# Layer 3's attention by two heads and a batch element, with projections between its steps and layer 2's last steps among the first of them

## The chip, the cores and the metric

The kernel runs on one core of a Trainium2 chip. The metric is the device time of one execution in microseconds: the median of three runs of the kernel before is 2154.16 us (2153.61 to 2156.42). The core's engines work side by side, each in its own order: TensorE (PE, its weight loads are PEld), VectorE (DVE), ScalarE (ACT), GpSimd (POOL), and SyncE (SP), which issues transfers.

## What is computed

Four layers of gated cross-attention and feed-forward on x, of shape (2, 1024, 256), with a context of 2 x 64 rows. The change lies between layer 2's attention and the end of layer 3's. The part of the reference that bears on it:

```python
x = x + tanh(g_xattn[2]) * _L2_xattn_ref(_layernorm(x), ctx, ctx, mask, ...)     # 16 heads of 16
x = x + tanh(g_ffn[2]) * _L2_ffn_ref(_layernorm(x), weight_q, weight_scale, bias)
x = x + tanh(g_xattn[3]) * _L3_xattn_ref(ctx, _layernorm(x), ...)
x = x + tanh(g_ffn[3]) * _L3_ffn_ref(_layernorm(x), ...)

# _L2_ffn_ref: each row of the normed x is quantised to int8
amax = max(abs(x2d), -1); x_scale = maximum(amax, 1e-6) / 127
x_q = clip(round(x2d / x_scale), -128, 127)
out = (x_q @ weight_q.T) * x_scale * weight_scale + bias

# _L3_xattn_ref(x=ctx, latents=normed x): 8 heads of 64
xn, zn = layer_norm(x, ...), layer_norm(latents, ...)
q = (zn @ Wq) heads; kv_in = concatenate([xn, zn], axis=1)      # 64 + 1024 keys
k, v = (kv_in @ Wk) heads, (kv_in @ Wv) heads
alphas = softmax(q * 64**-0.5 @ k.T)                             # 1024 queries x 1088 keys
return (alphas @ v) joined @ Wout
```

## The kernel before, in words

x lies in SBUF as 16 tiles of 128 rows (tiles 0 to 7 are batch element 0, tiles 8 to 15 are batch element 1). Inside the stages looked at here TensorE's order is the order of the program (`manual_schedule`); the orders of the other engines are made by a scheduler when the program is built. PSUM has eight banks. `banks(s, A)` sets how many are in the ring "s" (one bank each, taken in turn by `ps`) and how many tiles of two banks there are in "A" (`psA`); `evac` copies a bank to SBUF, in turn by DVE and by ACT.

**Layer 2's attention** (`ctx_attn`, from L530) runs one tile per step n. Its scores (L554) stand on TensorE at step n, the transposes of its exponentials two steps later, the product with the values three steps later, and the update of x four steps later. Steps of the layer that follows hang on it through `then`, a list of (lag, function): function f runs for tile n - lag at step n. For layer 2 these are the functions of `l2_ffn`: norm (statistics and, for every fourth tile, the normed rows xn of four tiles), quantised (the maximum, the scale, q on ACT, the clip on POOL, xq on ACT, and the bias added to x on POOL), turn (qtr, L1751, the transposes of four xq tiles, every fourth step), product (acc, the product with the int8 weights in bf16, and x updated), norms (two norms in one, on POOL, then zn of four tiles), and zturn (tr, L188, the transposes of four zn into zT). The lags are 4, 7, 8, 12, 13, 14. The loop ends at step 20; what is left of `then` is returned as a flat list of calls, `rest`.

**Layer 3's attention** is set up in `l2_l3_xattn`. `projected(b, o)` (from L1838) makes q, k, v of all eight heads for batch element b: with 512 columns of zT at a time, a product for each of four head pairs of q and of k (prj, L204), and v by tiles of 128 rows and 512 columns (v, L1858); kc and vc are the keys and values of the context, kcb a block form of kc in which two heads share one 128-wide operand. It is a generator; the projections of batch element 0 are run one by one between the calls of `rest` (L1872 to L1880), and those of batch element 1 stand between the two calls of `l3_heads`.

`l3_heads` (from L1888) takes one batch element in 32 steps: groups of two query tiles, and in a group four head pairs by two tiles. Step n does, on TensorE: the scores s of two heads (L1928, two tiles of "A", all of it), the first or second half of the values' product for an earlier tile pair (po, L1963), and the transposes et of the exponentials of step n - 1 (L1951, four banks of "s"). DVE takes the maxima (L1936, L1937) and half of the et copies, ACT the exponentials (L1938) and the other half. Once a group: `context` (sc, scores against the context, L1911), `shares` (L1975 to L1980: POOL adds, ACT takes the exponential, DVE sums it to r and inverts), `spread` (ecT; POOL copies r to rb, wide; R, L2001), `joined` (pc, L2016, and two DVE operations on half a group at a time), and `out` (wo, L2030: for each query tile four products added up in PSUM, then `add_gated`, L236, onto x). The pipeline runs out after 32 steps and starts again for the other batch element. After it layer 3's feed-forward takes the norm of all of x (L172 to L176).

Of the kernel before, what the change touches and what calls it, by code (L numbers as in the profile page):

```python
# [11 lines left out]
F32 = mybir.dt.float32  # L12
# [8 lines left out]
P = 128  # L21
# [19 lines left out]
class Net:  # L41
# [488 lines left out]
    def ctx_attn(self, pool, kbd, vblk, queries, extra, wo, gate, some=None, then=(), take=None):  # L530
# [57 lines left out]
        with tc.manual_schedule(engines={mybir.EngineType.PE}):  # L588
# [17 lines left out]
            partial(f, n - k)  # L606
            for n in range(last, NT + max([0] + [k + 1 for k, _ in then]))
            for k, f in then if 0 <= n - k < NT
# [335 lines left out]
    def l1(self, take, taken, back):  # L944
# [4 lines left out]
        with tc.tile_pool(name="l1f", bufs=1, side="right") as pool:  # L949
# [9 lines left out]
            with tc.tile_pool(name="l1a", bufs=1, side="right") as fp:  # L959
                es = ExitStack()  # L960
                f = self.l1_front(fp, es.enter_context(tc.tile_pool(name="l1q", bufs=1, side="right")), rows)
                rest = self.l1_xattn(f["steps"], take)
                taken()
                self.l1_attention(u, f, rest, es.close, ln2, oh, hbuf)
# [730 lines left out]
    def l2_ffn(self, pool, lw, zT):  # L1695
# [94 lines left out]
        return (4, norm), (7, quantised), (8, turn), (12, product), (13, norms), (14, zturn)  # L1790


    def l2_l3_xattn(self, late, take, taken):
# [4 lines left out]
        with ExitStack() as es:  # L1798
# [34 lines left out]
            qp = es.enter_context(tc.tile_pool(name="l3p", bufs=1))  # L1833

            kcb = qp.tile([P, 4, 2, L], F32, tag="kcb", name="kcb")
            nc.gpsimd.memset(kcb, 0.0)

            def projected(b, o):  # L1838

                zb = zT[:, :, b * S : (b + 1) * S]  # L1840
                cb = cT[:, :, b * L : (b + 1) * L]
                qT = o["qT"] = qp.tile([P, 4, S], F32, tag="qT", name="qT")
                kT = o["kT"] = qp.tile([P, 4, S], F32, tag="kT", name="kT")
                v = o["v"] = qp.tile([P, KM, 512], F32, tag="v", name="v")

                vc = o["vc"] = qp.tile([P, 512], F32, tag="vc", name="vc")
                for h in range(2):
                    t = slice(512 * h, 512 * h + 512)
                    for m in range(4):
                        self.project_T(wq[:, :, ts(m, P)], zb[:, :, t], qT[:, m : m + 1, t], scale=D3X**-0.5)  # L1850
                        yield
                        self.project_T(wk[:, :, ts(m, P)], zb[:, :, t], kT[:, m : m + 1, t])
                        yield
                    for t in range(4 * h, 4 * h + 4 + h):
                        p = self.ps("v")
                        for k in range(DC):
                            src = zb[:, k, ts(t, P)] if t < KM else c2[:, k, b]
                            nc.tensor.matmul(p, src, wv[:, k, :], start=k == 0, stop=k == DC - 1)  # L1858
                        self.evac(v[:, t, :] if t < KM else vc, p)
                        yield  # L1860
                for m in range(4):
                    p = self.ps("kc")
                    for k in range(DC):
                        nc.tensor.matmul(
                            p[:, :L], wk[:, k, ts(m, P)], cb[:, k, :], start=k == 0, stop=k == DC - 1
                        )
                    for h in range(2):
                        r = slice(64 * h, 64 * h + 64)
                        self.evac(kcb[r, m, h, :], p[r, :L])

            o = {}
            with tc.manual_schedule(engines={mybir.EngineType.PE}):  # L1872

                steps = projected(0, o)
                for n, f in enumerate(rest):
                    f()
                    if n >= 2:
                        next(steps, None)
                for _ in steps:
                    pass  # L1880
            fs.close()
            hp = es.enter_context(tc.tile_pool(name="l3h", bufs=1))
            self.l3_heads(hp, 0, o["qT"], o["kT"], kcb, o["v"], o["vc"], wo)
            for _ in projected(1, o):
                pass
            self.l3_heads(hp, 1, o["qT"], o["kT"], kcb, o["v"], o["vc"], wo)

    def l3_heads(self, pool, b, qT, kT, kcb, v, vc, wo):  # L1888
# [5 lines left out]
        KM, GS = S // P, 8  # L1894
        self.banks(s=3, A=2)
        G = S // 256
        e, eT, po, grp = {}, {}, {}, {}

        def context(g):

            q = grp[g] = dict(
                sc=pool.tile([P, 2, H3X, L], F32, tag="scs", name="scs", bufs=2),
                nmc=pool.tile([P, 2, H3X], F32, tag="nmc", name="nmc", bufs=2),
                nm=pool.tile([P, 2, H3X], F32, tag="nm", name="nm", bufs=2),
                rs=pool.tile([P, 2, H3X], F32, tag="rs", name="rs", bufs=2),
                oT=pool.tile([P, 4, 256], F32, tag="oT", name="oT"),
            )
            for t in range(2):
                p = self.ps("sc")
                for c in range(4):  # L1910
                    nc.tensor.matmul(  # L1911
                        p[:, ts(c, P)], qT[:, c, ts(2 * g + t, P)],
                        kcb[:, c].rearrange("p h l -> p (h l)"), start=True, stop=True,
                    )
                nc.scalar.copy(q["sc"][:, t].rearrange("p h l -> p (h l)"), p)
# [419 lines left out]
```

## Time and profile before

| | us |
|---|---|
| median of three runs | 2154.16 |
| the profiled execution | 2174.95 |
| its span, first to last instruction | 2173.2 |
| layer 2's attention, first to last scores on TensorE | about 1190 to 1273 |
| first and second projection of batch element 0 on TensorE | 1309.35, 1312.03 |
| first head scores of batch element 0 | 1380.63 |
| projections of batch element 1 on TensorE | 1650.67 to about 1694 |
| first head scores of batch element 1 | 1698.01 |
| layer 3's last wo begins | 1959.13 |
| first normed row xn of the feed-forward | 1966.10 |
| mean granted clock of TensorE, share of full | 0.923 |

How to read the profile: the page gives each engine's busy time and the costliest groups of instructions, with the mean duration and what ended the idle time before them. The view by stage gives the busy time of each engine between two times, with the granted clock. The timeline lists instructions in order of time: start, duration, engine, line, operation, output and inputs, how many in a row, and in brackets the idle time just before and what ended it. A product of 32-bit operands stands as two passes in the trace, so four products of s are x8; a transpose is one.

### The profile page before, as it was taken

Reading aid. Unit: us, or ns where it says so; the run is one execution under the profiler, and the core shown is the slowest. Engines: PE = TensorE matmul, PEld = TensorE weight load, DVE = VectorE, ACT = ScalarE, POOL = GpSimd, SP = SyncE. Lnnn points to the kernel's source line nnn. Section 1 sums busy time; section 2 is a strip of 40 time slices with the busy share of each in tenths; the row PEclk is TensorE's granted clock in tenths of the full one; section 3 lists DMA queues with packets and bytes.
Section 4 is the critical chain, followed back from the end, with each engine's and each line's share of the span. In section 5 each row is a group of like instructions: output and inputs, shape, how many; then the busy total and the mean of one; then the engine's idle time right before and its main releaser. Section 6 shows DMA issues by size and latency. Waiting matters only on the chain.

```text
span 2173.2 us, 26234 instructions
## 1 busy us (share of the span) xinstructions
PE 1847.3 (85%) x9627; PEld 1163.8 (54%) x9627; DVE 1116.5 (51%) x2437; ACT 840.8 (39%) x1603; POOL 425.0 (20%) x652
## 2 busy tenths in 40 slices
PE   7839999599688898994895978799999899998884
PEld 3437777377445454542553754455655555565553
DVE  6750010656777647723345763356662455656434
ACT  4302222455434564571112654354442444441121
POOL 1013331211421121113331233000000000000462
PEclk9959999799889999995997968799999999998997
DMA  4032331300000000007432300000000000002234
GB/s 146 20 117 89 113 121 60 115 1 1 7 2 2 1 12 2 11 11 269 154 131 84 98 1 0 0 1 1 1 1 1 1 1 1 1 1 87 60 91 155
DMA packets 70603, 107.09 MB, mean 49 GB/s; under 512 B 13779, under 2 KB 55382, under 8 KB 70214
## 3 DMA queue, kind: packets, MB, share of 16 engines
q1 hardware_dynamic: 54582, 63.17, 8.8%
q0 software_dynamic: 13824, 40.55, 5.6%
q8 instruction: 81, 1.33, 0.3%
q10 hardware_dynamic: 2064, 1.62, 0.2%
q14 instruction: 52, 0.43, 0.1%
HBM read 80.90 MB, written 24.15 MB: 48 GB/s over the span
## 4 chain that ended last, share of the span: by engine, by line
PE 50%; DVE 11%; issue 6%; ACT 6%; POOL 5%; DMA 4%; SPq 1%; ACTq 0%; POOLq 0%; DVEq 0%
PE s L1928 6%; PE et L1951 4%; PE po L1963 4%; PE po L1257 3%; PE s L1187 3%; PE prj L204 3%; PE po L352 3%; PE sT L1238 3%; DVE nm L1193 2%; PE h L2102 2%; DVE nm L1936 2%; DMA ybuf<-yo,si 2%; PE v L1858 1%; PE s L554 1%; PE wo L2030 1%
## 5 line engine op out<-in xcount | busy, mean ns | idle before, releaser
L1193 DVE TENSOR_REDUCE nm<-s 128x1 f32<-128x512 f32 (+3 forms) x304 | 184.2, 656 | 68.7 <-PE s L1192 46.8
L1938 ACT ACTIVATE e<-s,nm 128x1024 f32<-128x1024 f32 x128 | 141.5, 1111 | 179.9 <-DVE nm L1937 88.5
L1936 DVE TENSOR_REDUCE nm<-s 128x1 f32<-128x1024 f32 x128 | 150.8, 1220 | 99.0 <-PE s L1928 99.0
L1246 ACT ACTIVATE eT<-sT 128x512 f32<-128x512 f32 x288 | 148.9, 602 | 112.6 <-PE sT L1238 81.5
L1928 PE MATMUL s<-kT,qT 64*128 64x512 f32 x512 | 162.3, 639 | 11.2 <-ACT e L1938 11.2
L1951 PE MATMUL et<-ident,e 128*128 128x128 f32 x1024 | 139.9, 283 | 17.2 <-DVE eT L112 12.4
L1187 PE MATMUL s<-kT,qT 128*128 128x512 f32 (+3 forms) x384 | 129.7, 418 | 16.5 <-ACT qT L114 9.5
L1951 PEld LDWEIGHTS et<-ident,e 128*128 128x128 f32 x1024 | 113.7, 144 | 54.1 <-issue 22.2
L1963 PE MATMUL po<-eT,v 128*64 128x256 f32 x1024 | 125.6, 385 | 0.3 <-DVE eT L112 0.2
L1187 PEld LDWEIGHTS s<-kT,qT 128*128 128x128 f32 x384 | 73.3, 197 | 81.8 <-DVE nm L1193 27.1
L791 PE MATMUL h<-xeT,w 128*128 128x384 f32 (+1 forms) x416 | 110.3, 424 | 0.7 <-PEq L844 0.4
L112 DVE COPY eT<-et 128x512 f32<-128x512 f32 x128 | 87.9, 687 | 40.5 <-PE et L1951 40.1
L795 ACT ACTIVATE hT<-h,b 128x384 f32<-128x384 f32 (+1 forms) x104 | 53.0, 510 | 138.4 <-PE h L791 117.8
L801 DVE TENSOR_TENSOR y<-yp,b 128x256 f32<-128x256 f32 (+1 forms) x34 | 14.4, 423 | 178.8 <-PE yp L809 178.2
L1963 PEld LDWEIGHTS po<-eT,v 128*64 128x64 f32 x1024 | 68.5, 136 | 69.4 <-issue 32.3
L1975 POOL TENSOR_TENSOR ec<-scs,nm 128x1024 f32<-128x1024 f32 x8 | 15.2, 1904 | 460.9 <-DVE nm L1937 415.3
L809 PE MATMUL yp<-w,hT 128*128 128x256 f32 x464 | 102.8, 380 | 0.0
L1238 PE MATMUL sT<-qT,kT 128*128 128x512 f32 x288 | 96.9, 451 | 1.8 <-DMA qT<-mT 1.8
L1928 PEld LDWEIGHTS s<-kT,qT 64*128 64x128 f32 x512 | 59.1, 191 | 71.5 <-ACT e L1938 35.5
L809 PEld LDWEIGHTS yp<-w,hT 128*128 128x128 f32 x464 | 87.7, 190 | 15.5 <-issue 2.1
L791 PEld LDWEIGHTS h<-xeT,w 128*128 128x128 f32 x416 | 71.1, 193 | 36.3 <-issue 5.3
L1626 PE MATMUL up<-w,xT 128*128 x152 | 77.2, 632 | 14.2 <-DVE ub L1630 7.0
(495 smaller groups left out, 3577.1 us busy)
## 6 DMA issues: line engine op xcount, KB each, us to landing
w<-in_L_ffn_W_dram SPq DMA_DIRECT2D x24, 1024.0 KB, 8.4
y<-ybuf SPq DMA_DIRECT2D x20, 512.0 KB, 4.5
ybuf<-zero POOLq DMA_DIRECT2D x8, 512.0 KB
hbuf<-xn SPq DMA_DIRECT2D x32, 128.0 KB, 1.8
w<-in_L_ffn_W_dram SPq DMA_DIRECT2D x8, 512.0 KB, 9.3
x<-in_x_dram SPq DMA_DIRECT2D x16, 128.0 KB, 4.5
hbuf<-hn SPq DMA_DIRECT2D x16, 128.0 KB, 1.7
L_ffn_w1T<-in_L_ffn_w1T_dram SPq DMA_DIRECT2D x1, 2048.0 KB, 7.8
```

What stands on the lines that cost most here:

```text
L112: self.nc.vector.tensor_copy(out, in_)
L791: nc.tensor.matmul(p[:, :m], W[e][0][:, k, ts(hc, P)], X[e][:, k, r : r + m], start=k == 0, stop=k == DC - 1,)
L809: nc.tensor.matmul(p[:m, :D], hT[:, hc, r : r + m], W[e][1][:, hc, :], start=hc == 0, stop=hc == HC - 1,)
L1187: nc.tensor.matmul(o, qT[:, h0 + j, :], kT[:, (h0 + j) // 4, b * S + k0 : b * S + k0 + m], start=True, stop=k0 + m < n,)
L1193: nc.vector.tensor_reduce(nm[:, u, h0 : h0 + nh], s[:, : nh * m].rearrange("p (h k) -> p h k", h=nh), AX.X, ALU.max, negate=True,)
L1238: nc.tensor.matmul(s, kT[:, kv, b * S + kt * P : b * S + (kt + 1) * P], qT[:, 4 * kv : 4 * kv + 4, :], start=True, stop=kt < qt,)
L1246: nc.scalar.activation(eT[:, kv, :], s, AF.Exp)
L1928: nc.tensor.matmul(s[h][:, ts(u, 512)], qT[r, c, ts(2 * g + t, P)], kT[r, c, ts(u, 512)], start=True, stop=True,)
L1936: nc.vector.tensor_reduce(m, s[h], AX.X, ALU.max, negate=True)
L1938: nc.scalar.activation(e[n][h], s[h], AF.Exp, bias=m, accum_out=q["rs"][:, t, j])
L1951: nc.tensor.transpose(p[:, ts(j, P)], e[n][h][:, ts(k + j, P)], self.ident)
L1963: nc.tensor.matmul(po[j][64 * h : 64 * h + 64, :256], v[:, k, ts(2 * c + h, D3X)], eT[j][h][:, k, :], start=k == 0, stop=k == KM - 1,)
```

## The change

Three things are changed.

The steps of layer 2's feed-forward get smaller lags. quantised, product and norms are called for two tiles at once at steps in which a group of four is complete (`two`): the lags are norm 4, quantised 4 and 5, turn 6, product 7 and 8, norms 8 and 9, zturn 11. `rest` becomes a list of lists, one for each step (layer 1, which uses the same function, makes it flat again).

`l3_heads` and `projected` are replaced by `l3_attention`. A group is now two heads (a head pair c) of one batch element, and its eight steps are the eight query tiles. The eight groups run in one loop of 64 steps and a drain of eight, in the order (0, b0), (1, b0), (0, b1), (1, b1), (2, b0), (3, b0), (2, b1), (3, b1). The projections of the next group (two q, two k, kc, two v, and, with a batch element's first group, vc for all its heads) are put one by one ahead of the transposes of each step; v is made for 128 columns at a time. `out` multiplies one head pair by its rows of Wout and adds to x at once, so that each x tile is updated four times, in place of four products added up in PSUM. R is made of r directly, half by half, without the copy rb. oT, ecT and R lie in a pool that is opened when `rest` is empty, after layer 2's pool is closed.

Layer 2's remaining steps (`rest`) stand between the first projections and in steps 0 to 3 of the loop; the PSUM banks are in the form of layer 3 (three in "s") from before they run.

```diff
         return [
-            partial(f, n - k)
+            [partial(f, n - k) for k, f in then if 0 <= n - k < NT]
             for n in range(last, NT + max([0] + [k + 1 for k, _ in then]))
-            for k, f in then if 0 <= n - k < NT
         ]
...
-                rest = self.l1_xattn(f["steps"], take)
+                rest = sum(self.l1_xattn(f["steps"], take), [])
...
-        return (4, norm), (7, quantised), (8, turn), (12, product), (13, norms), (14, zturn)
+        def two(f, first):
+            def both(i):
+                if i % 4 == 3:
+                    for j in (0, 1):
+                        f(i - 3 + first + j)
+            return both
+
+        return (
+            (4, norm), (4, two(quantised, 0)), (5, two(quantised, 2)), (6, turn), (7, two(product, 0)),
+            (8, two(product, 2)), (8, two(norms, 0)), (9, two(norms, 2)), (11, zturn),
+        )
...
+        self.banks(s=3, A=2)
+        order = [(c + d, b) for c in (0, 2) for b in range(B) for d in range(2)]
+        kcb = pool.tile([P, 4, B, 2, L], F32, tag="kcb", name="kcb")
+        nc.gpsimd.memset(kcb, 0.0)
+        vc = pool.tile([P, B, 512], F32, tag="vc", name="vc")
+
+        def projected(g):
+            c, b = order[g]
...
+            for k, m, scale in (("qT", wq, D3X**-0.5), ("kT", wk, None)):
                 for h in range(2):
                     t = slice(512 * h, 512 * h + 512)
+                    self.project_T(m[:, :, ts(c, P)], zb[:, :, t], q[k][:, :, t], scale=scale)
+                    yield
...
+            for t in range(0, KM, 4):
+                p = self.ps("v")
+                for j in range(4):
                     for k in range(DC):
                         nc.tensor.matmul(
+                            p[:, ts(j, P)], zb[:, k, ts(t + j, P)], wv[:, k, ts(c, P)],
+                            start=k == 0, stop=k == DC - 1,
                         )
+                self.evac(q["v"][:, t : t + 4, :].rearrange("p t d -> p (t d)"), p)
+                yield
...
         def spread(g):
...
-            rb = pool.tile([P, 2, H3X, D3X], F32, tag="ec", name="rb")
-            nc.gpsimd.tensor_copy(rb, q["r"][:, :, :, None].to_broadcast([P, 2, H3X, D3X]))
...
+                for t in range(4):
+                    for h in range(2):
+                        nc.tensor.matmul(
+                            p[ts(h, 64), ts(t, P)],
+                            q["r"][:, 4 * u + t, h : h + 1].to_broadcast([P, D3X]), self.ident,
+                            start=True, stop=True,
+                        )
...
+        def out(g, u):
+            c, b = order[g]
+            y = self.ps("wo")
+            for t in range(2):
+                nc.tensor.matmul(
+                    y[:, ts(t, D)], grp[g]["oT"][:, ts(2 * u + t, P)], wo[:, c, :], start=True, stop=True
+                )
+            for t in range(2):
+                self.add_gated(b * SB + 2 * u + t, y[:, ts(t, D)], 3)
+
+        G = len(order)
         with self.tc.manual_schedule(engines={mybir.EngineType.PE}):
+            steps = projected(0)
+            rest = [r for r in rest if r]
+            for k in range(5):
+                for f in rest.pop(0) if k % 2 == 0 and rest else ():
+                    f()
+                next(steps)
             context(0)
+            for n in range(G * GS + GS):
+                g, t = divmod(n, GS)
+                if g < G:
                     scores(n)
+                if n >= 3 and (n - 3) // 2 < G * GS // 2:
                     values((n - 3) // 2, (n - 3) % 2)
+                if t == 6 and g + 1 < G:
+                    context(g + 1)
+                if g > 0:
+                    for d, f in ((0, shares), (1, spread), (3, joined)):
+                        if t == d:
+                            f(g - 1)
+                    if t >= 4:
+                        out(g - 1, t - 4)
+                for f in rest.pop(0) if rest else ():
+                    f()
+                if not rest and not late:
+                    late["pool"] = rest_done()
+                if g == 0 and t < 3:
+                    next(steps, None)
+                if t == 0 and g + 1 < G:
+                    nxt = projected(g + 1)
+                if g + 1 < G and t < 7:
+                    next(nxt)
+                if t == 7 and g + 1 < G:
+                    next(nxt, None)
                 if 1 <= n <= G * GS:
                     turn(n - 1)
         self.banks()
```

## The prediction

> **What bounds the kernel now.** I read the page first, then the busy time by stage from layer 2's attention on, then TensorE's timeline of that stretch, and last all engines in one step of layer 3's attention. The first 1190 us and everything after 1966 us are untouched, so only the stretch between is worked on.
>
> ```profile
> span 2173.2 us, 26234 instructions
> PE 1847.3 (85%) x9627; PEld 1163.8 (54%) x9627; DVE 1116.5 (51%) x2437; ACT 840.8 (39%) x1603; POOL 425.0 (20%) x652
> ```
>
> ```profile
> core 0: us, PE busy (x) PEld busy (x) DVE busy (x) ACT busy (x) POOL busy (x), PEclk, DMA share, GB/s
> 1276.00:1309.00 33.00, 21.23 (x103) 17.93 (x103) 15.00 (x59) 17.01 (x31) 13.52 (x22) 0.52 0.00 1
> 1309.00:1380.60 71.60, 57.46 (x180) 28.99 (x180) 23.59 (x67) 27.71 (x53) 20.31 (x40) 0.86 0.00 0
> 1380.60:1650.80 270.20, 246.26 (x1554) 154.37 (x1554) 158.20 (x257) 124.09 (x227) 11.76 (x8) 0.97 0.00 1
> 1650.80:1696.00 45.20, 44.68 (x117) 20.63 (x115) 7.50 (x15) 10.88 (x21) 0.00 (x0) 1.00 0.00 0
> 1696.00:1966.10 270.10, 250.88 (x1568) 153.21 (x1568) 158.57 (x268) 126.31 (x230) 13.34 (x31) 0.99 0.01 2
> ```
>
> These rows are the end of layer 2's attention, its last steps with batch element 0's projections, 32 head steps, batch element 1's projections, 32 head steps. No DMA runs. The head steps have TensorE over 91% busy, but its busy time hides waiting:
>
> ```profile
> 1746.97 1.99 PE L1928 MATMUL s<-kT,qT 64*128 64x512 f32 x8
> 1748.89 1.95 PE L1963 MATMUL po<-eT,v 128*64 128x256 f32 x16
> 1750.77 2.10 PE L1951 MATMUL et<-ident,e 128*128 128x128 f32 x16
> 1752.79 3.07 PE L1928 MATMUL s<-kT,qT 64*128 64x512 f32 x8
> ```
>
> The same eight passes take 1.99 us, and 3.07 us when the second score tile still waits for its exponential. A step with nothing else is s 1.92, po 1.88, et 2.03: 5.83 us. From the end of s the chain is two maxima (2.36), two small minima (0.28), two exponentials at 1.10 pitch: the tile that s needs next is free 4.8 us after, while po and et fill 3.9. Eight steps (1767.88 to 1832.04) take 64.2 us for 57.4 us of TensorE work: 46.6 plus sc 1.98, wo 3.65, ecT 1.09, R 2.05, pc 1.95.
>
> Ahead of the heads TensorE waits for layer 2's chain through POOL and ACT, and runs slowly after each wait:
>
> ```profile
> 1252.37 0.38 PE L1751 MATMUL qtr<-identb,xq 128*128 128x128 bf16 x4 [2.03 <-ACT eT L576]
> 1253.11 1.98 PE L554 MATMUL s<-kbd,qT 64*128 64x256 f32 x8
> 1267.05 1.13 PE L554 MATMUL s<-kbd,qT 64*128 64x256 f32 x8
> 1300.67 2.80 PE L188 MATMUL tr<-ident,zn 128*128 128x128 f32 x8 [6.11 <-ACT zn L163]
> 1325.21 3.53 PE L204 MATMUL prj<-zT,L_xattn_Wk 128*128 128x512 f32 x4 [5.93 <-ACT qT L219]
> 1375.02 2.80 PE L188 MATMUL tr<-ident,zn 128*128 128x128 f32 x8 [7.01 <-ACT zn L163]
> ```
>
> After the 2.03 us wait the scores take 1.98 instead of 1.13 us and the slow rows go on for some 8 us: about 4 us lost besides the wait.
>
> **The front.** Layer 2's lags shrink, so TensorE meets xq two steps after norm instead of four. In the trace, group 0's last x is updated at 1223.95 and POOL's norm chain ends at 1227.2. The built order of the changed program then puts on ACT: four xn, the step's eT copies and exponentials, q, xq; and on POOL four bias adds (0.73 each) ahead of four clips (1.07). With the trace's durations the last xq comes at about 1241.6; TensorE arrives at 1238.0. So a wait of 3.6 us and 4 us of slow clock replace the 2.0 us wait at 1250. Groups 1 and 2 come out alike by the same walk: waits of 4.2 and 6.3 us, each slow after. zn needs POOL's second chain (4.1 us) and ACT's four rows (2.1), both queued behind the clips, and lands near TensorE's arrival. Layer 2's attention so ends at 1308, as now. Layer 2's last steps then run with three "s" banks instead of four; beside waits of 4 to 6 us for POOL I set that to nothing (between nothing and one ACT copy, 0.6, for each of its eight qtr tiles). Group 3 still needs its chain: q projections 1313, a wait for xq to 1320.6, k projections, products and zturn to 1329, kc and sc 2.5. The first s is at about **1332** instead of 1380.6. With no waits the work alone puts it at 1305; one more wait of 7 us with its slow clock puts it at 1345.
>
> The Trainium skill, "TensorE: Matmul & The Clock Gate", section "Part 1: The HAM clock gate", says half clock comes only after an idle window of some 3.4 us and ends after as much activity. The row above has it after 2.03 us of idling and for 8 us, so the row decides; by the page each wait would lose 1.7 us instead of 4, and the first s would come some 9 us sooner.
>
> **A head step after.** Per group (two heads, one batch element, eight query tiles) TensorE does 46.6, sc 1.98, ecT 1.02, pc 1.90, wo 3.65 as before. New in it: q and k projections 4 x 1.72 = 6.87, kc 0.47, and v as 16 products of 128 columns: sc has this shape, 8 in 1.98, so 3.96 (3.43 at today's width). R becomes 32 passes with 64-column weights; the nearest rows are today's R (16 passes 2.05) and the weight loads of po (16 in 1.49). Ends 2.05 (halves paired) and 4.1 (not); I take 3.0 from po's loads. POOL's rb copy and TensorE's wait for it (1.22 per group) go. Work is **69.6 us** per group.
>
> The same skill page, section "LDWEIGHTS (loading the stationary operand)", prices a load by its columns, 53 ns for 64; po's loads in this trace average 136 ns and start 93 ns apart. By the page R would be 1.7 us, 10 us less in all.
>
> Every step now has 0.9 us or more of extra work, so the 4.8 us chain no longer ends last. Late next is the ring of three PSUM banks "s", which the projections now share with et: the built order puts the exponentials (4.5 to 6.75 us after the step's start) on ACT ahead of every copy, so a bank that ACT empties comes free at 7.4 to 7.7, and the third allocation after it waits. Walking the eight steps with their work and end: t=0 7.55 becomes 9.85 (q's bank 1.2; also r's reduction sits on DVE ahead of the maxima, 1.05, as at 1755.8 now); t=1 11.57; t=2 7.55 becomes 8.23; t=3 9.5; t=4 7.23 becomes 8.36 (half of kcb is copied by ACT); t=5 8.74; t=6 10.72 becomes 11.95 (v needs sc's bank); t=7 6.9. Sum **75.1 us**, 5.5 of it waiting. DVE has 158.2/4 = 39.6 now, plus 6 x 0.484 (add_gated on eight tiles, not two) and 1.6 of copies, 44 us; ACT 124.1/4 = 31.0 plus 2.6 of copies: neither bounds. The oT, ecT and R pool opens after layer 2's tiles are dropped (step 3; first used in step 4): nothing. kcb's memset doubles to 1.05 on POOL and is hidden by group 3's chain. No DMA is added or moved: layer 3's weights have landed by 1250, and the loads behind the heads (SP, 1963.36) move with their end.
>
> **The sum**, against the profiled execution. First group, without spread, joined and out, with v, vc (1.72) and layer 2's last steps: 64.3. Six groups 450.6, vc 1.7. Last group, no projections: 60.3. Drain to xn: now 22.9 from the 32nd step (1943.2 to 1966.1); less 1.2 for rb, plus 1.0 for R, plus eight tiles' add_gated and statistics after the last group instead of two, 3.8: 26.5. So 1332 + 64.3 + 450.6 + 1.7 + 60.3 + 26.5 = 1935 against 1966: **31 us less**. Seen the other way: a group costs what it costs now with its share of projections (64.2 + 43.5/4 = 75.1), so the inside brings nothing. The gain is one drain and refill fewer (1629 to 1651 and 1698 to 1713) and the earlier start, less the projections of batch element 0 that now lie inside.
>
> The profiled execution took 2174.95 us (2173.2 of span), 1% above the median of 2154.16; taken off the median, the same 31 us give **2123**.
>
> **Rivals.** (1) *TensorE's work alone decides*: the copies come off before the banks return. Then 5.5 x 7 = 39 us more are gained: 2084. For it: et waits only 17 us in all 64 steps today; against it, today four et have the ring to themselves. (2) *The front gives nothing*: chains of about 18 us per group of four tiles run one after another with the clock halved, and the first s slips from 1332 to 1363 or later. About 2153. For it: four waits of 6 to 7 us today. Against: chains of neighbouring groups overlap attention steps. (3) *Slower*: the bank ring becomes the bound of every step. If the five steps that I walked with little or no wait lose 1.2 us each as t=4 and t=6 do, a group is 81 us, and seven groups (the first and the last counted by halves) lose 42: 2165. It decides from 75.1 + 31/7 = 79.5 us a group, 9.9 a step. For it: DVE has eight add_gated that hold wo banks. Against: DVE is 60% busy and the extra products themselves give ACT time. (4) *It does not interleave*: the built order has projections in every step, so I leave it out.
>
> **Chances.** Forecast 0.55, (1) 0.18, (2) 0.13, (3) 0.14. 0.2% (4.3 us) is about what a measurement can tell. Of (2) 0.04 fall faster, 0.06 within, 0.03 slower: faster 0.77, same 0.06, slower 0.17. The unknowns: start 1305 to 1345 (-27, +13), waits from none to double (-39, +39), R (-8, +9), hardly all at one end: 2085 to 2155, which leaves out most of (3) and the lower half of (1).
>
> **What would show it.** Right: first s near 1332; groups of 75 us with every step over 6.8; s at 1.9 to 2.1 us instead of 3.07; et or prj idle before "ACT" copies some 5 us a group; xn at about 1934. Wrong: steps over 10 us with et waiting for ACT in most (rival 3); groups of 70 us (rival 1); qtr and tr waits over 10 us or a first s after 1360 (rival 2). R's rows price the 64-column loads.

## The result and the profile after

The changed kernel takes 2132.77 us (median of four runs, 2131.77 to 2136.01) against 2155.29 (2153.61 to 2161.74) for the kernel before, run beside it: a ratio of 0.989, 95% interval 0.9867 to 0.9912. That is 22.5 us less. 2123 was predicted, with a range of 2085 to 2155; 31 us less were expected, and the likeliest case is the one that came.

The profiled execution took 2133.59 us. Two lines of its page, the span with its instructions and the busy time of each engine:

```profile
span 2131.8 us, 26729 instructions
PE 1812.5 (85%) x9860; PEld 1153.0 (54%) x9883; DVE 1133.4 (53%) x2485; ACT 840.6 (39%) x1603; POOL 417.0 (20%) x644
```

The shares are those of before: an average over the whole span doesn't show what happened. The view by stage does. First before, then after, each cut at the same three events: the first mask scores of layer 2's attention, the first head scores, the first xn of layer 3's feed-forward, the end. (The columns are the busy times of the engines, then the granted clock, the DMA share and the GB/s.)

```profile
1190.13:1380.63 190.50, 159.98 (x821) 106.86 (x819) 104.39 (x278) 96.49 (x169) 52.32 (x89) 0.84 0.09 28
1380.63:1966.10 585.47, 541.80 (x3237) 328.22 (x3236) 324.23 (x540) 261.29 (x478) 25.10 (x39) 0.98 0.01 2
1966.10:2173.20 207.10, 158.18 (x700) 108.57 (x700) 98.05 (x237) 38.01 (x102) 76.38 (x78) 0.88 0.32 102
```

```profile
1197.57:1341.98 144.41, 115.23 (x713) 82.63 (x712) 93.22 (x259) 85.27 (x147) 49.21 (x80) 0.86 0.11 37
1341.98:1946.81 604.83, 554.12 (x3601) 340.75 (x3600) 352.84 (x606) 271.58 (x500) 20.40 (x40) 0.99 0.02 5
1946.81:2131.80 184.99, 150.96 (x700) 106.92 (x700) 98.36 (x237) 38.66 (x102) 76.36 (x78) 0.88 0.32 102
```

The front is 46.1 us shorter and the heads are 19.4 longer: 26.7 less in the stretch that the change touches (775.97 to 749.24). The two profiles differ by 41.4 us in all, because the untouched ends differ too: 7.4 more ahead of layer 2's attention, 22.1 less behind xn, with the same 700 instructions on TensorE. So the profiled pair can't be subtracted as a whole; the stretch can. It is the measure in what follows.

Inside the heads the steady group of eight steps takes 74.63 us (the starts of the 32nd, 40th, 48th and 56th step are 1641.25, 1715.88, 1790.50 and 1865.12). Rows of the first of these groups, from TensorE's timeline:

```profile
1641.25 1.99 PE L1940 MATMUL s<-kT,qT 64*128 64x512 f32 x8
1649.71 1.09 PE L1962 MATMUL et<-ident,e 128*128 128x128 f32 x8 [1.81 <-ACT qT L219]
1655.55 1.97 PE L2010 MATMUL R<-ident,r 128*64 128x128 f32 x32
1658.12 1.98 PE L204 MATMUL prj<-zT,L_xattn_Wq 128*128 128x512 f32 x4 [0.60 <-ACT ecT L114]
1704.94 2.05 PE L1900 MATMUL v<-L_xattn_Wv,zT 128*128 128x128 f32 x16 [1.67 <-DVE nmc L1928]
```

s takes 1.99 us in all eight steps of this group; in the group of before that the prediction adds up (1767.88 to 1832.04) it took 3.0 to 3.07 in four of the eight. Its second tile is now free in time. In exchange et, prj and v wait for banks. ACT's timeline in the first of these steps shows why the bank of the q projection (made by 1646.9) is late:

```profile
1646.59 1.11 ACT L1949 ACTIVATE e<-s,nm 128x1024 f32<-128x1024 f32 x1 [3.66 <-DVE nm L1948]
1647.70 1.10 ACT L1949 ACTIVATE e<-s,nm 128x1024 f32<-128x1024 f32 x1
1648.79 0.37 ACT L1982 COPY oT<-po 128x256 f32<-128x256 f32 x1
1649.04 0.61 ACT L219 ACTIVATE qT<-prj 128x512 f32<-128x512 f32 x1
```

The copy is behind two exponentials and oT, and ends at 1649.65, just ahead of the et that waited for it.

### The profile page after: what moved, and what is told of

It is laid out like the page before. It is cut to its first block, busy times and chain, and to the rows that moved or that the text cites. A ratio compares the mean times of both kernels' runs of the same rounds, so it can differ in the third digit from the quotient of the medians.

```text
span 2131.8 us, 26729 instructions
## 1 busy us (share of the span) xinstructions
PE 1812.5 (85%) x9860; PEld 1153.0 (54%) x9883; DVE 1133.4 (53%) x2485; ACT 840.6 (39%) x1603; POOL 417.0 (20%) x644
## 4 chain that ended last, share of the span: by engine, by line
PE 44%; DVE 13%; ACT 8%; issue 6%; POOL 5%; DMA 3%; SPq 2%; ACTq 0%; POOLq 0%; DVEq 0%
PE s L1940 5%; DVE nm L1947 4%; PE et L1962 4%; PE s L1186 4%; PE po L1256 3%; PE sT L1237 3%; ACT e L1949 3%; PE prj L204 3%; PE h L2131 2%; PE po L1974 2%; DVE nm L1192 2%; PE po L352 2%; DMA ybuf<-yo,si 2%; SPq L1580 1%; PE s L554 1%
## 5 line engine op out<-in xcount | busy, mean ns | idle before, releaser
L1940 PE MATMUL s<-kT,qT 64*128 64x512 f32 x512 | 131.9, 623 | 0.0
L1988 POOL TENSOR_TENSOR scs<-scs,nm 128x1024 f32<-128x1024 f32 x8 | 15.2, 1904 | 555.3 <-DVE nm L1948 555.3
L800 DVE TENSOR_TENSOR y<-yp,b 128x256 f32<-128x256 f32 (+1 forms) x34 | 14.4, 423 | 177.3 <-PE yp L808 176.7
L790 PEld LDWEIGHTS h<-xeT,w 128*128 128x128 f32 x416 | 70.5, 191 | 35.4 <-issue 3.4
L114 ACT COPY eT<-et 128x512 f32<-128x512 f32 x128 | 74.2, 591 | 37.9 <-PE et L1962 37.7
```

Source lines behind the costliest of these rows:

```text
L790: nc.tensor.matmul(p[:, :m], W[e][0][:, k, ts(hc, P)], X[e][:, k, r : r + m], start=k == 0, stop=k == DC - 1,)
L1940: nc.tensor.matmul(s[h][:, ts(u, 512)], q["qT"][r, 0, ts(t, P)], q["kT"][r, 0, ts(u, 512)], start=True, stop=True,)
```

## The experiments

Each kernel's time is set against the kernel before on the same chip; chips differ (before took 2156.08 on one, 2179.33 and 2176.98 on two others). The changed kernel itself was timed on the first chip alone, so the others are set against it through their ratios to before and through the stretch of one profile each. From each profile: the front, from layer 2's first mask scores to the first head scores; a steady group; the heads, from the first head scores to xn; and the stretch, front and heads together.

| kernel | us | before there | ratio, 95% interval | front | group | heads | stretch |
|---|---|---|---|---|---|---|---|
| before | 2155.29 | | | 190.50 | 64.2 | 585.47 | 775.97 |
| before_again | 2182.48, one run | 2179.33 | | 189.04 | 64.2 | 580.62 | 769.66 |
| after | 2132.77 | 2155.29 | 0.989 (0.9867 to 0.9912) | 144.41 | 74.63 | 604.83 | 749.24 |
| lags_only | 2175.82 | 2179.33 | 0.9982 (0.9967 to 0.9997) | 183.83 | 64.2 | 585.39 | 769.22 |
| old_lags | 2162.95 | 2179.33 | 0.9935 (0.9911 to 0.9959) | 158.07 | 74.6 | 599.60 | 757.67 |
| rest_first | 2166.07 | 2179.33 | 0.9932 (0.9906 to 0.9957) | 164.54 | 74.6 | 599.14 | 763.68 |
| block | 2216.12 | 2156.08 | 1.0266 (1.0218 to 1.0314) | 149.95 | 88.6 | 684.22 | 834.17 |
| q_on_dve | 2120.74 | 2156.08 | 0.9838 (0.9816 to 0.9859) | 146.39 | 72.72 | 593.72 | 740.11 |
| sc_split | 2124.60 | 2156.08 | 0.9849 (0.9831 to 0.9867) | 148.35 | 73.43 | 597.71 | 746.06 |
| clip_on_dve | 2130.65 | 2156.08 | 0.9876 (0.9857 to 0.9894) | 143.56 | 74.64 | 606.02 | 749.58 |
| block_step2 | 2148.25 | 2176.98 | 0.9875 (0.984 to 0.991) | 143.06 | 73.0 | 596.42 | 739.48 |
| two_loops | 2162.68 | 2176.98 | 0.9935 (0.9912 to 0.9958) | 148.20 | 74.6 | 609.00 | 757.20 |
| q_and_split | 2130.08 | 2176.98 | 0.9772 (0.9727 to 0.9817) | 144.94 | 71.5 | 586.27 | 731.21 |
| all_on_dve | 2121.14 | 2176.98 | 0.974 (0.9708 to 0.9772) | 146.40 | 70.5 | 573.62 | 720.02 |

**before_again**: the kernel before, with no edit.

> The kernel before, unchanged, profiled a second time. In the first pair of profiles the stretch from layer 2's first mask scores to the first xn of layer 3's feed-forward is 775.97 us before and 749.24 after (26.7 less), the stretch ahead of it 1190.13 and 1197.57 (7.4 more), the stretch behind it 207.1 and 185.0 (22.1 less). My theory: the change acts in the middle stretch alone; then this run shows 776 +-1 there, and the stretch behind it, whose code is the same in both, is somewhere between 185 and 207 by chance. Rival: the change shortens what follows it; then this run shows 207 behind it again.

The stretch took 769.66, not 776 +-1: two profiles of one kernel differ by 6.3 us in it, 4.4 of them in the first head group (60.25 and 55.83). Against the two the change saves 20.4 to 26.7 us, and the 22.5 of the runs lie between. What is behind xn took 214.0. In the fourteen profiles it is 185 to 188 us in five and 205 to 214 in nine, and the nine include kernels with the changed code. All nine are from the two slower chips, but for the first profile of before, which took some 20 us more than its own other runs. The change doesn't shorten it.

**Where the front's 46 us come from.** Three kernels take the front apart.

lags_only, edited in the kernel before (with `two` as in the change):

```diff
-        return (4, norm), (7, quantised), (8, turn), (12, product), (13, norms), (14, zturn)
+        return (
+            (4, norm), (4, two(quantised, 0)), (5, two(quantised, 2)), (6, turn), (7, two(product, 0)),
+            (8, two(product, 2)), (8, two(norms, 0)), (9, two(norms, 2)), (11, zturn),
+        )
```

> The kernel before with the change's smaller lags for layer 2's steps and nothing else of it. If the lags alone give the earlier front, layer 2's last steps are over sooner, batch element 0's projections (45 us of work) are nearly all that is left behind 1309, and the first head scores come at about 1355 instead of 1380.6 (counted from the same start of layer 2's attention): 25 us less, some 2130. If it is the rest running beside the projections and head steps that gives it, the lags bring 0 to 8 us: 2147 to 2155.

old_lags, edited in the changed kernel:

```diff
-        return (
-            (4, norm), (4, two(quantised, 0)), (5, two(quantised, 2)), (6, turn), (7, two(product, 0)),
-            (8, two(product, 2)), (8, two(norms, 0)), (9, two(norms, 2)), (11, zturn),
-        )
+        return (4, norm), (7, quantised), (8, turn), (12, product), (13, norms), (14, zturn)
...
-                for f in rest.pop(0) if k % 2 == 0 and rest else ():
+                for f in sum((rest.pop(0) for _ in range(2 if k == 0 else 1)), []):
                     f()
```

> The changed kernel with the old lags (4, 7, 8, 12, 13, 14); the longer rest is spread over the same places (two steps of it ahead of the first projection, one ahead of each further one, the others in head steps 0 to 3). If the lags alone give the front, the first head scores slip by 25 us: about 2158. If the rest beside the projections gives it, they come 0 to 8 us later than in the changed kernel (1342 in its profile): 2133 to 2141. The head groups keep their 74.6 us by either.

rest_first, edited in the changed kernel:

```diff
-            for k in range(5):
-                for f in rest.pop(0) if k % 2 == 0 and rest else ():
-                    f()
-                next(steps)
+            for f in sum(rest, []):
+                f()
+            rest = []
+            for _ in range(5):
+                next(steps)
```

> The changed kernel with all of layer 2's remaining steps run before the first projection, so that nothing of TensorE's covers group 3's chain. My theory: the chain through POOL and ACT ends when it did (last zT at about 1339), then five projections, kc and sc, 11 to 14 us with a slow clock, stand behind it: first scores at 1350 to 1353 instead of 1342, and the first group is 4 us shorter for the work that has gone from it: 4 to 8 us slower, 2137 to 2141. Rival: the rest in the head steps was hidden anyway and the first group's waits go with it: 2130 to 2134.

The lags alone give 5.2 us (6.7 against the first profile), at a ratio of 0.9982: the case "0 to 8 us". With the rest deferred, the old lags cost 13.7 us of front, more than the 0 to 8 of my theory and less than the 25 of the rival; 5.2 of these come back in the heads, whose first group is 3.8 us shorter. rest_first loses 20.1 us of front, where 8 to 11 were expected, and gets 5.7 back; a net loss of 14.4 by its stretch, where 4 to 8 were expected (9 by the ratios: its profiled execution was the slowest of seven, 12 us above their median). So neither part does it alone. In order, the front is 189 to 190 us in before; 183.8 with the smaller lags; 164.5 when only five projections, not all of batch element 0's, stand ahead of the first scores; 144.4 when the rest runs beside the projections and the first head steps. The last two steps are worth 18 to 20 us each (the front of like kernels spreads over 143 to 150, so each of these figures is good to some 3 us). They are not what is gained, since projections that leave the front come back in the heads. By the stretch the smaller lags give 0.4 to 6.7 us, the new loop with the rest ahead of it 5.5 more, and the rest beside the projections and the first head steps 14.4 more; by the ratios it is 4, 11 and 9. So each of the last two parts is worth some 5 to 14 us, and no run here says it closer.

**Does spreading the projections gain anything inside?** block, edited in the changed kernel:

```diff
-                if g + 1 < G and t < 7:
-                    next(nxt)
-                if t == 7 and g + 1 < G:
-                    next(nxt, None)
+                if t == 0 and g + 1 < G:
+                    for _ in nxt:
+                        pass
```

> The changed kernel with all projections of the next group in one block in step 0 of a group, instead of one in each step. My theory that a group costs the same either way (the steps without extra work have their 4.8 us chain from s to the exponentials again, and s at 3.07): block 11.3 us of work and 0.5 of waits, plus a group without projections, 64.2 less the 1.2 that the rb copy cost: 74.8 us a group, 2133 +-5. Rival 1: spreading fills the waits and is the gain: a block then costs 3 us or more a group, 2154 and up. Rival 2: spreading costs more in bank waits than it fills: 70 to 72 a group, 2105 to 2118.

A group took 88.6 us, 14 more, as if spreading were a large gain. TensorE's timeline behind the block speaks of something else:

```profile
1523.37 0.66 PE L1962 MATMUL et<-ident,e 128*128 128x128 f32 x4 [0.79 <-DVE eT L112]
1524.70 0.66 PE L1962 MATMUL et<-ident,e 128*128 128x128 f32 x4 [0.68 <-ACT eT L114]
1550.54 1.95 PE L1974 MATMUL po<-eT,v 128*64 128x256 f32 x16
1553.85 1.72 PE L1962 MATMUL et<-ident,e 128*128 128x128 f32 x12 [0.77 <-DVE v L112]
```

and DVE's timeline:

```profile
1553.11 0.69 DVE L112 COPY v<-v 128x512 f32<-128x512 f32 x1
```

Every et of four transposes waits for the copy of the et before it: a ring of one bank. The two v banks, filled from 1518.36 on, are copied only at 1553.11 (ACT's at 1554.28). v has two buffers, and the older of them is read by the values of the group before until step 2 (the po at 1550.54); until then v's banks can't be emptied. The edit had added a hold of its own. Moved behind that:

```diff
-                if t == 0 and g + 1 < G:
+                if t == 2 and g + 1 < G:
```

> The changed kernel with all projections of the next group in one block in step 2 of a group, behind that step's values. In the block of step 0 the two v banks could not be emptied until the group before had used its v (step 2), and one bank was left for et: 88.6 us a group. In step 2 that hold is gone. Theory that a group costs the same with its projections spread or in a block: 64.2 less the 1.2 of the rb copy, plus 11.3 of projections and 0.5 of waits: 74.8 a group, 0.989 of before, within 5 us of the changed kernel. Rival: a block starves DVE and ACT of the maxima and exponentials behind its copies: 77 us a group and up, 17 us or more slower than the changed kernel.

A group takes 73.0 us with the block in step 2 and 74.63 spread, and the ratio is 0.9875 against 0.989, within the intervals. So spreading, as it is done here, gains nothing inside; it is even 1.6 us a group behind a well placed block. Its waits for banks eat what it fills.

**two_loops**: one drain and refill more. The loop over n runs twice, for groups 0 to 3 and 4 to 7:

```diff
-            context(0)
-            for n in range(G * GS + GS):
-                g, t = divmod(n, GS)
-                if g < G:
-                    scores(n)
...
+            for first in (0, G // 2):
+                end = first + G // 2
+                context(first)
+                for n in range(first * GS, end * GS + GS):
+                    g, t = divmod(n, GS)
+                    if g < end:
+                        scores(n)
...
```

> The changed kernel with its one loop over eight groups cut in two loops of four, so that the pipeline drains and starts again once, as in the kernel before (the projections of the fifth group still stand in the steps of the fourth). Theory, from the rows of before: its fourth and fifth group took 128.36 and 54.78 us around 45.2 of projections, 9.6 more than two groups of 64.2, so the cut costs about 10 us: 0.9935 of before. Rival: TensorE is idle for only 1.0 us in the changed kernel's own drain (1924.79 to 1941.87 with 16.1 of work), and the refill's waits take the place of bank waits that go: 0 to 4 us, 0.989 to 0.991 of before.

The fourth and fifth group took 89.86 and 64.36 us, 154.2 against 149.3: the cut costs 5.0 us, and the heads are 4.2 longer. That is half of the theory's 10 and just above the rival's 0 to 4. The ratio (0.9935, 4.5 thousandths over that of the changed kernel) would put it at 10 us, but the two intervals touch, and 3.8 us of the stretch's 8.0 lie in the front, where nothing was edited. A drain and refill less is worth some 5 us; the gain is mostly the front's.

**Whose copy holds the bank?** q_on_dve, edited in the changed kernel:

```diff
-                    self.project_T(m[:, :, ts(c, P)], zb[:, :, t], q[k][:, :, t], scale=scale)
+                    p = self.ps("prj")
+                    for kk in range(DC):
+                        nc.tensor.matmul(
+                            p, m[:, kk, ts(c, P)], zb[:, kk, t], start=kk == 0, stop=kk == DC - 1
+                        )
+                    if scale is None:
+                        nc.vector.tensor_copy(q[k][:, 0, t], p)
+                    else:
+                        nc.vector.tensor_scalar(q[k][:, 0, t], p, scale, None, ALU.mult)
```

> The changed kernel with DVE, not ACT, emptying the banks of the q projections and all of the k projections. My theory that a bank waits because ACT's copy stands behind two exponentials: step 0 loses its wait of 1.81 us before et, step 2 its 0.44; step 1's 0.60 (ecT on ACT) and the others stay: 2.2 us a group less, 72.4, some 14 to 17 us in all: 2116 to 2119. Rival: DVE's maxima are what decides, and four copies more on DVE (2.7 us a group) put them later: 74.6 to 77 a group, 2133 to 2150.

In step 0 of a steady group DVE has done its maxima, and copies the product as soon as it is there. The sixteen et follow without a wait:

```profile
1638.57 2.20 PE L1970 MATMUL et<-ident,e 128*128 128x128 f32 x16
```

```profile
1638.77 0.69 DVE L1893 TENSOR_SCALAR qT<-prj 128x512 f32<-128x512 f32 x1 [0.46 <-PE prj L1887]
```

Step 0 goes from 9.48 to 7.74 us and step 2 from 8.24 to 7.75; steps 1 and 3 get longer by 0.16 and 0.15. A group is 1.91 us shorter (2.2 expected), the ratio 0.9838. The wait was ACT's order.

sc_split, edited in the changed kernel (`context` makes its tiles on the first call and one half of sc on each):

```diff
-                if t == 6 and g + 1 < G:
-                    context(g + 1)
+                if t in (5, 6) and g + 1 < G:
+                    context(g + 1, (t - 5,))
```

> The changed kernel with the first half of sc in step 5 and the second in step 6, instead of both in step 6. My theory: step 6 loses its wait of 1.67 us for sc's bank and 0.95 of work, step 5 gains 0.95 of work and no wait: 1.7 us a group less, 73.0, some 11 us in all: 2122. Rival: the wait moves to the et of steps 5 and 6, since each of them still takes seven banks: 74.6 a group, 2133.

Step 5 goes from 8.52 to 9.73 us, step 6 from 12.24 to 9.84: 1.2 a group, not 1.7 (a wait of 0.34 for sc's bank is left, now before et); 0.9849.

q_and_split has both edits.

> The changed kernel with both edits that cut bank waits alone: q and k emptied by DVE (74.63 to 72.72 us a group) and sc's halves in steps 5 and 6 (74.63 to 73.43). Theory: the waits lie in different steps and add: 71.5 us a group, 20 us less than the changed kernel, 0.980 of before. Rival: the second finds the chain from s to the exponentials behind the wait it removes: 72.7 a group, 0.984.

They add: 71.5 us a group as the theory had it, and 18.0 us less in the stretch.

all_on_dve has also the other new copies on DVE (four lines; the first and the last of them):

```diff
-                self.evac(kcb[r, c, b, h, :], p[r, :L])
+                nc.vector.tensor_copy(kcb[r, c, b, h, :], p[r, :L])
...
-                self.evac(q["ecT"][:, ts(u, 512)], p)
+                nc.vector.tensor_copy(q["ecT"][:, ts(u, 512)], p)
```

> As the last one, and kcb, v, vc and ecT are emptied by DVE as well, so that of the new copies none stands behind ACT's exponentials (R and et still alternate). Theory: step 1 loses its 0.60 us for ecT, step 4 its 0.85 for kcb, and the first group 3 to 4 of its 3.58 us for v: 10 to 14 us less than with the two edits, 70.1 a group, 0.974 to 0.976 of before; this is the rival of the prediction in which TensorE's work alone decides. Rival: DVE, 48 us busy of 71 by then, puts the maxima behind these copies: 71.5 a group or more, 0.980 or more.

70.48 us a group, the stretch at 720.02, a ratio of 0.974 (0.9708 to 0.9772): 29.2 us less in the stretch than the changed kernel, with the same work on TensorE. It beats both kernels. Step 1 of one of its groups, in which TensorE waits for nothing:

```profile
1628.31 1.99 PE L1949 MATMUL s<-kT,qT 64*128 64x512 f32 x8
1630.23 1.95 PE L1983 MATMUL po<-eT,v 128*64 128x256 f32 x16
1632.11 1.09 PE L2013 MATMUL ecT<-ident,scs 128*128 128x128 f32 x8
1633.13 1.97 PE L2019 MATMUL R<-ident,r 128*64 128x128 f32 x32
1635.03 1.98 PE L1887 MATMUL prj<-zT,L_xattn_Wq 128*128 128x512 f32 x4
1636.85 2.20 PE L1971 MATMUL et<-ident,e 128*128 128x128 f32 x16
```

From start to start these come to 10.67 us; step 1 of the changed kernel, with the same instructions, takes 11.18. The page of this kernel has 1158.1 us of DVE and 816.7 of ACT against 1133.4 and 840.6: what was taken off ACT costs little on the path (steps 5 and 6 together take 0.5 us more than in q_and_split).

**clip_on_dve**: the front's chain. Edited in the changed kernel:

```diff
-            gp.tensor_scalar(q, q, MAGIC - 128.0, MAGIC + 127.0, ALU.max, ALU.min)
+            nc.vector.tensor_scalar(q, q, MAGIC - 128.0, MAGIC + 127.0, ALU.max, ALU.min)
```

> The changed kernel with the clip of layer 2's quantisation on DVE instead of POOL. In group 3 the fourth clip stood on POOL behind a norm chain of 3.7 us (xq waits until 1331); in the others POOL's 1.1 us a row paces the xq that qtr waits for. My theory: DVE, idle half of that time, does a clip in 0.4 to 0.5 us, the last xq of group 3 comes at 1326, the waits of groups 0 to 2 (2.55, 4.2, 3.5) shrink by about half, and the slow clock after them with it: first scores at 1327 to 1336 instead of 1342: 6 to 15 us less, 2118 to 2127. Rival: ACT's order (xn, q and xq behind exponentials) paces the chain, and nothing moves: 2131 to 2134.

The reason for trying it stands in POOL's timeline of the changed kernel: group 3's last clip is behind group 2's norm chain.

```profile
1325.68 0.23 POOL L146 TENSOR_SCALAR n_r<-mv 128x4 f32<-128x4 f32 x1
...
1329.11 0.20 POOL L1774 TENSOR_TENSOR n<-n,n_r 128x4 f32<-128x4 f32 x1
1329.39 1.07 POOL L1738 TENSOR_SCALAR q<-q 128x256 f32<-128x256 f32 x1
```

On DVE a clip takes 0.29 us, not 1.07, and group 3's last qtr starts 129.4 us after layer 2's first scores instead of 133.5. But the front is 143.56 instead of 144.41, where 6 to 15 less were expected. Two rows of qtr, of groups 1 and 3:

```profile
1278.87 0.71 PE L1750 MATMUL qtr<-identb,xq 128*128 128x128 bf16 x5 [4.75 <-ACT xq L1740]
1325.25 0.71 PE L1750 MATMUL qtr<-identb,xq 128*128 128x128 bf16 x5 [0.18 <-ACT xq L1740]
```

Group 1 waits longer than it did (4.75 after 2.55, against 3.35 and 0.85). Behind group 3's qtr the two k projections take 8.4 us, where they took 5.1 in the changed kernel. The second of them waits 1.07 us for the copy of xqT, which ACT makes only after four zn rows, and all of it runs at a granted clock of 0.50, against 0.68. So of the 4.1 us gained at qtr 0.85 are left at the first head scores. The waits fit the rival, that ACT's order sets the pace once POOL's share is gone; what is lost to the slow clock neither of the two had counted. My theory of this experiment was wrong by its size.

## Why the prediction was right, and where it was not

**The front.** The first head scores were put at 1332, 141.9 us after layer 2's first scores; they came at 144.4. Eight profiles with the same front, or nearly (the changed kernel and those experiments that edit only the heads), have 143.1 to 150.0, 146.5 in the mean. The walk held roughly: waits for xq of 2.6, 4.2 and 3.5 us in groups 0 to 2 (3.6, 4.2 and 6.3 predicted), the first projection 118.9 after the first scores (1308 predicted, 117.9). What came late was group 3: xq was given until 1320.6 and came 3.0 us later by the same count, since POOL had the norm chain of group 2 ahead of the last clip. The walk had each group's clips but not a neighbour's chain among them. That chain alone didn't set the front, though: in clip_on_dve the same qtr comes at 129.4, and the first head scores still come at 143.6.

**The slow clock** was put at 4 us of loss after each of the first three waits, after one place of before. There TensorE works without a gap from 1252.4 on, and has half clock from 1253.25 to about 1263.5:

```profile
1253.25:1261.50 8.25, 8.25 (x36) 6.52 (x36) 4.03 (x11) 4.59 (x10) 1.80 (x2) 0.50 0.00 0
```

That is 10 us at half speed, 5 us lost. After the wait of equal length for group 0's xq in the changed kernel:

```profile
1250.00:1253.30 3.30, 3.30 (x16) 1.88 (x16) 0.00 (x0) 1.84 (x3) 0.00 (x0) 0.55 0.29 104
1253.30:1257.00 3.70, 3.70 (x13) 1.79 (x11) 2.45 (x2) 1.67 (x3) 0.00 (x0) 1.00 0.00 0
```

Half clock for some 3 us of work loses 1.5 us; after the waits that end at 1279.88 and 1331.06 it lasts 3.8 us each. The Trainium skill ("TensorE: Matmul & The Clock Gate", "Part 1: The HAM clock gate") has full clock back after some 3.4 us of activity: near that in these three places, and not in the one of before. Nor is it so around group 2's waits (2.65, 0.85 and 2.06 us), where 11.5 us of work ran at half clock:

```profile
1300.75:1317.82 17.07, 11.49 (x52) 9.33 (x52) 7.23 (x25) 8.20 (x15) 8.55 (x16) 0.50 0.00 0
```

So half clock cost 1.5, 1.9 and 5.7 us after the three waits, 9.1 in place of 12: too much for two of them and too little for the third. The waits for xq of groups 0 to 2 were 10.3 in place of 14.1. Against these 7 us stand some 8 that I had left out: waits of 2.06 for xqT and 1.45 for eT, group 3's 3 us, and 1.7 of half clock at 1235.9, where I had no wait. That they nearly cancel is luck.

**The group**: 75.1 predicted, 74.63 measured. By steps, predicted and measured: 9.85 and 9.48, 11.57 and 11.18, 8.23 and 8.24, 9.5 and 9.46, 8.36 and 8.43, 8.74 and 8.52, 11.95 and 12.24, 6.9 and 7.08. The causes named were the right ones: q's bank in step 0, kcb's in step 4, sc's in step 6 wait as said, and q_on_dve, sc_split and all_on_dve take these waits away, all but 0.34 us of sc's. That the inside brings nothing is shown by block_step2.

**R** was mis-sized: 3.0 us, from po's loads. In the last group, where nothing waits behind it, it took 1.90 from its start to the next product's, 59 ns for each of 32 passes, though each load is listed at 132 to 137 ns:

```profile
L2010 PEld LDWEIGHTS R<-ident,r x256: 132/137/137, 1429.6 to 1933.5; 128*64 128x64 f32 x128
```

So the listed duration of a load is no pitch. The row that decided was po's, whose loads are as wide and start 93 ns apart; its passes carry 256 columns and R's 128. Sixteen passes of po take 1.88 us, 117 ns each, twice a pass of R. Since the loads are alike, po's pitch comes from the columns that a pass carries, not from its load; which of the two sets R's, no run here tells apart. The Trainium skill ("TensorE: Matmul & The Clock Gate", "LDWEIGHTS (loading the stationary operand)") prices a load of 64 columns at 53 ns; the estimate of 1.7 us for R from it was nearer. v was given 3.96 and takes 3.67. From start to start the rows of a group come to 68 us of work (46.2 for s, po and et of eight steps, 7.3 for q and k, 0.4 kc, 3.7 v, 1.9 each for sc, R and pc, 1.0 ecT, 3.9 wo), not 69.6 (69.5 by the terms as they are printed), and leave 6.6 of waiting, not 5.5: two errors that nearly cancel, which is luck too.

**The ends of the heads.** The first group was put at 64.3 and took 71.11. I had walked it without waits for banks; et waits 3.58 us for a v that ACT empties late, and 1 us or less in several other places. In all_on_dve, with v, k and kcb among the copies on DVE, the group takes 65.94. The middle groups with vc were put at 452.3 and took 452.03 (79.6, 73.9 and four times 74.6), the last group at 60.3 and took 59.67. The drain was put at 26.5 and took 22.02, no more than the 22.9 of before: R costs nothing more, and eight add_gated for the last group go beside the wo that feed them. 6.8 too little and 4.5 too much, again by luck of opposite signs: the heads were put at 603 and took 604.83.

So the sum was off by 4.3 us (26.7 in place of 31): 2.5 in the front, 1.8 in the heads. The other 4 us between 26.7 and the 22.5 of the runs are within what two profiles of the same code differ by.

**The rivals.** (1), that TensorE's work alone decides, was not this kernel's case but is nearly that of all_on_dve: 29 us of the 39 that it was said to be worth. What keeps the changed kernel from it is the choice of the engine that empties the banks and the two halves of sc in one step. (2), that the front gives nothing, had the first head scores at 1363 or later, 173 us after layer 2's first scores; they came at 144.4, so the chains do overlap. (Of the four waits of 6 to 7 us named for it, the trace of before shows three: 6.11, 5.93 and 7.01.) (3), a ring that bounds every step, needed 79.5 us a group; steps 2, 3, 5 and 7 wait 0.7 us or less. block, by accident, shows rival (3) at work: one bank for et, and 88.6 us a group.

## What to carry to other kernels

Work put between the steps of a pipeline costs the bank it passes through for as long as its copy waits: look at what stands ahead of that copy on its engine, and at whether its target buffer is free, before counting what the work fills. A copy that any engine can do belongs on the one that is free when the bank is full: here DVE has done its two maxima by then, while ACT still has two exponentials ahead of it. Six kinds of copies moved off ACT, with sc in two halves, were worth as much again as the whole rearrangement (29.2 us of the stretch, against 20.4 to 26.7). And to take an edit apart, cut the profile at the events that it touches: the untouched ends moved by more than the change did.

## What the runs showed that I had not expected

Half clock can come behind waits far shorter than a few microseconds, and with a delay. TensorE stood for 0.62 us at 1233.0 and then worked on without a gap; the clock was full until 1235.9 and then 0.66 in the mean of 5 us:

```profile
1235.90:1240.90 5.00, 5.00 (x29) 3.33 (x26) 4.06 (x12) 3.99 (x8) 3.56 (x6) 0.66 0.30 96
```

That the wait did it is not shown: TensorE stood for 1.19 us at 1264.7 as well, and the clock stayed full until 1276.9. Nor does one and the same wait always do it. The wait for q's bank is 1.74 us in the second group and 1.80 or 1.81 in the fourth to seventh: after it the granted clock was 0.69 for 4.4 us in the second group and s took 3.35 us, while in the fifth it stayed at 1.00 and s took 1.99.

How long half clock lasts varied from 3 to 10 us of steady work. It doesn't take just any length, though. The traces of all fourteen profiles record only full and half clock, and every stretch of half clock, but the last one that reaches beyond the kernel's end, is a whole number of 3.41 us long, from one of them to fifteen. So the work lost depends on where in such a stretch a wait ends. What starts a stretch and what ends it, no run here shows.

The 20 us by which the code behind xn varies without any change in it also stay open. In its longer form (the second profile of before) TensorE idles 6.6 and 5.3 us ahead of the two kinds of y and 2.6 ahead of up, put down to nothing but issue; in the profile of q_on_dve these are not there.
